# A post-norm transformer layer: the first feed-forward matmul on ternary weights and split activations, and a new order of the small pieces

## The chip, the core and the metric

One core of one Trainium2 chip. The metric is the device time of one execution, in microseconds, as the median of several. All input tensors start in device memory (HBM), and the output of shape 8 x 1024 x 256, fp32, ends there. The names used below: PE is the matmul engine (PEld its weight loads), DVE the vector engine, ACT the scalar (activation) engine, POOL the general engine, SP the engine whose queue issues nearly all DMAs.

## The reference

```python
# x: 8 x 1024 x 256; 16 heads of 16
Q, K, V = split_heads(x @ Wq.T + bq), split_heads(x @ Wk.T + bk), split_heads(x @ Wv.T + bv)
scores = einsum('bhqd,bhkd->bhqk', Q, K) / sqrt(16) + prior_lambda * gaussian_mask(1024)
out = einsum('bhqk,bhkd->bhqd', softmax(scores), V)       # heads joined again
x = layernorm(x + out @ Wo.T + bo)

def bitlinear(x, w):
    scale = clip(mean(abs(w), axis=1, keepdims=True), 1e-5, None)
    return x @ (clip(round(w / scale), -1, 1) * scale).T
h = bitlinear(x, w_fc) + gate * (x @ v.T @ fast_b.T @ u.T)  # w_fc 1024 x 256; rank 16
r = maximum(h, 0)
x = layernorm(x + bitlinear(r * r, w_proj))                 # w_proj 256 x 1024
```

So the first feed-forward matmul has two parts. The weights of the large part have only the values -1, 0 and 1, times one scale for each of the 1024 hidden rows. The second part goes through rank 16.

## The kernel before

**Groups.** The attention runs in 512 groups, 64 for each of the 8 batches. In one group PE forms two score tiles that are ready for the exponential (`exp_scores`, L684; matmuls at L699), then some other pieces of work, then the four matmuls (L629, `max_scores`) whose row maxima are needed 12 groups later, and at last the product of the previous group's exponentials with V (L738, `weigh`). In five of eight groups the Gaussian mask touches the tile: there the first of the two tiles gets four matmuls with the mask (L709), and DVE adds it to the second (L722). ACT takes the exponentials (L723). DVE takes the row maxima, two for each group, 1024 columns each (L641, `max_row`); one of them is queued before the pieces' results are taken out of PSUM, the other only in the next group. Scores live in three PSUM tiles of two banks each that are taken in turn.

**Pieces.** Everything else is cut into pieces that a scheduler in Python puts into the groups while the program is built: for the batch after, `transpose_x`, `queries_keys` and `values`; for the batch before, the feed-forward part in four chunks of 256 rows (`chunk`, L819). A chunk is two `project` pieces (output projection, residual, statistics of the norm), two `turn` pieces (transposing x), eight `hidden` pieces (first feed-forward matmul, L884), and four half `output` pieces (L918). A piece writes half a PSUM bank, `misc`, of which there are two halves, so that a group takes two such pieces at most. A piece is a tuple: an assumed PE cost, the function, the number of halves, and a condition. The loop at L1072 pays out credit: each group gets its share of the batch's total cost, and pieces are taken while there is credit. `defer(n, f)` puts work n groups later; it is issued by `run_deferred` (L1133), before the pieces' results are taken.

**What is computed how.** Matmul operands of type F32R go through PE once, plain F32 operands in several passes (two records in the trace for each matmul). The scores and the second feed-forward matmul already use pairs of F32R numbers, the value rounded and the rest. The first feed-forward matmul is plain F32: `prepare_fc` (L407) forms in batch 0 the whole weight, ternary value times scale plus the low-rank product, in `wfT`; `hidden` multiplies it with `x1T`. The square of the relu is then split in `hi` and `lo`: ACT relu (L896) and square (L900), POOL multiplication (L901) and subtraction (L903; on DVE in the last batch).

**Queues.** All instructions of an engine run in the order in which they were issued (L1146 to L1151 add that dependency). SP's DMAs stand in one such order too: the q and k parts (L189 to L196), the row maxima's round trip through HBM (L671, L677), the sums and outputs of the attention (L756, L759), the steps of the softmax normalization (L764 to L793: `sums`, `invert`, `fetch`, `divide`, deferred by 1, 2, 3 and 4 groups) and the loads.

**Tail.** After group 511 the last batch's feed-forward part runs alone (L1139), on the score tiles' PSUM banks, which `early` (L363) hands out in pairs.

Of the kernel before, what the change touches and what calls it, by code (L numbers as in the profile page):

```python
# [16 lines left out]
P = 128  # L17
# [21 lines left out]
def tile_postln_layer(  # L39
# [82 lines left out]
    ones = cpool.tile([P, P], F32, tag="ones", name="ones")  # L122
# [97 lines left out]
    for name in "kq":  # L220
# [3 lines left out]
        p1.tile([P, HALF], F32, tag="full", name="full_0"),  # L224
        p1.tile([P, HALF], F32, tag="avs", name="full_1"),
        p2.tile([P, HALF], F32, tag="rl", name="full_2"),
        p2.tile([P, HALF], F32, tag="rl", name="full_3"),
# [5 lines left out]
    first_part("q", qscale, 0, "rec", fulls[1])  # L233
# [95 lines left out]
    gate_c = cpool.tile([R, 1], F32, tag="gate", name="gate_c")  # L329
    nc.sync.dma_start(gate_c, gate.partition_broadcast(R))  # L330
    fb_sb = cpool.tile([R, R], F32, tag="fb", name="fb_sb")
    nc.sync.dma_start(fb_sb, fast_b)
    v_sb = cpool.tile([R, D], F32, tag="v_sb", name="v_sb")
    nc.sync.dma_start(v_sb, v)
    u_sb = cpool.tile([P, NHC, R], F32, tag="u_sb", name="u_sb")
# [48 lines left out]
    wfT = cpool.tile([P, NDC, FF], F32, tag="wfT", name="wfT")  # L384
# [3 lines left out]
    def scales(w, n, name):  # L388


        sc = p2.tile([P, 3], F32, tag="sc", name=f"sc_{name}")
        nc.vector.tensor_reduce(
            out=sc[:, 0:1], in_=w, axis=AX.X, op=ALU.add, apply_absolute_value=True
        )
        nc.vector.tensor_scalar(sc[:, 0:1], sc[:, 0:1], 1.0 / n, 1e-5, op0=ALU.mult, op1=ALU.max)
        nc.vector.tensor_scalar_mul(sc[:, 1:2], sc[:, 0:1], 0.5)
        nc.vector.tensor_scalar_mul(sc[:, 2:3], sc[:, 0:1], -0.5)
        return sc

    def ternary(w, sc, name):  # L400

        t = p1.tile([P, D], F32, tag="tern", name=f"tern_{name}")
        nc.gpsimd.tensor_scalar(t, w, sc[:, 2:3], None, op0=ALU.is_lt)
        nc.gpsimd.tensor_scalar(w, w, sc[:, 1:2], None, op0=ALU.is_gt)
        nc.gpsimd.tensor_sub(w, w, t)

    def prepare_fc(half):  # L407

# [25 lines left out]

        def second():
            st["a"] = p1.tile([R, HALF], F32, tag="lo", name=f"a_{half}")
            pas = [misc(f"pa_{half}_{k}") for k in range(2)]
            for k, pa in enumerate(pas):
                nc.tensor.matmul(
                    pa[:R, :], fb_sb, st["uT"][:, ts(k, D)], start=True, stop=True  # L440
                )

            def empty():
# [12 lines left out]
        def piece(i):  # L456
# [13 lines left out]
            def empty():  # L470
# [3 lines left out]
                if i + 1 < n:  # L474
                    tern(i + 1)
# [723 lines left out]
```

## Time and profile before

Three runs took 2405.73, 2407.56 and 2408.98 us, median 2407.56. The profiled execution took 2407.72 us, of which 2405.8 us are the span from the first to the last instruction.

| stretch of the span (us) | what runs | length | PE busy | DVE busy | ACT busy | POOL busy | PE clock |
|---|---|---|---|---|---|---|---|
| 0 to 70 | weights, first q, k, v, first maxima | 70 | 46.96 | 41.69 | 12.62 | 23.88 | 0.79 |
| 70 to 332 | batch 0, and preparing the feed-forward weights | 262 | 244.14 | 196.39 | 143.60 | 63.33 | 0.98 |
| 604 to 883 | batch 2 | 279 | 274.79 | 197.51 | 162.16 | 93.53 | 0.99 |
| 1716 to 1998 | batch 6 | 282 | 277.04 | 198.36 | 162.24 | 93.54 | 0.99 |
| 1998 to 2267 | batch 7 | 269 | 260.50 | 168.55 | 159.31 | 92.33 | 0.99 |
| 2320 to 2347 | tail, second chunk | 27 | 18.33 | 7.98 | 6.11 | 13.62 | 0.81 |

Busy is the time in which an engine had at least one instruction in work. The clock is what was granted to PE, as a share of full speed. The costs of instructions that the change touches, as the page's groups give them (busy us in all, mean ns of one): L884 228.8 and 383 (896 records), L896 on `misc` 83.5 and 382 (224), L850 23.2 and 415 (56), L594 18.3 and 611 (30 each for q and k), L789 40.3 and 1281 (32). PE, DVE and the others wait for each other through semaphores; in the profile a wait stands as idle time before an instruction, with the instruction that ended it.

### The profile page before, as it was taken

What the parts mean: (1) busy time and instruction counts of PE and PEld (TensorE: products, weight loads), DVE (VectorE), ACT (ScalarE), POOL (GpSimd) and SP (SyncE); (2) the same over time, 40 slices, a digit from 0 to 9 for tenths busy, and PEclk for the clock granted to TensorE, in tenths of its full rate; (3) what the DMA queues carried; (4) which work ended last, traced back from release to release, by engine and by line L of the source; (5) the groups of instructions that cost most, each with busy time, mean ns of one, the idle gap of its engine ahead of it and who ended that gap; (6) DMA issues with size and microseconds to landing.
All of it is one profiled execution on the core that took longest, in us unless ns stands there. A gap on an engine that the chain in (4) does not pass through costs nothing.

```text
span 2405.8 us, 35921 instructions
## 1 busy us (share of the span) xinstructions
PE 2269.3 (94%) x12956; PEld 1302.4 (54%) x12956; DVE 1623.2 (67%) x3117; ACT 1312.0 (55%) x1748; POOL 790.1 (33%) x796
## 2 busy tenths in 40 slices
PE   6899999999999999999999999999999999999666
PEld 4444445555555555555555555555555555555344
DVE  6677777777677777677676776777766777776122
ACT  1455565655555565665556555555655556555421
POOL 3124112323223342333324332333323333333344
PEclk8899999999999999999999999999999999999878
DMA  8223343231423323132423223233332124221100
GB/s 207 74 66 102 73 110 100 63 77 44 130 85 83 86 79 112 56 84 69 119 85 102 68 55 111 86 85 79 94 111 65 59 73 117 65 50 33 37 13 18
DMA packets 108433, 194.06 MB, mean 81 GB/s; under 512 B 20944, under 2 KB 49888, under 8 KB 108256
## 3 DMA queue, kind: packets, MB, share of 16 engines
q1 hardware_dynamic: 106848, 189.68, 28.7%
q10 hardware_dynamic: 1408, 2.10, 0.3%
q8 instruction: 102, 1.67, 0.3%
q14 instruction: 75, 0.61, 0.1%
HBM read 105.73 MB, written 85.98 MB: 80 GB/s over the span
## 4 chain that ended last, share of the span: by engine, by line
PE 76%; DVE 10%; DMA 5%; POOL 3%; issue 3%; ACT 1%; SPq 1%; POOLq 0%; DVEq 0%; ACTq 0%
PE e L699 19%; PE av L738 16%; PE s L629 14%; PE misc L884 7%; DVE junk L641 7%; PE e L709 5%; PE misc L918 5%; PE misc L575 4%; DMA o<-raw_o 2%; PE misc L553 2%; PE misc L841 2%; DVE st L798 1%; DMA st_q<-parts_q 1%; PE py L918 1%; PE ph L884 1%
## 5 line engine op out<-in xcount | busy, mean ns | idle before, releaser
L641 DVE CUSTOM_DVE_ANT_0 junk<-s,wide 128x1024 f32<-128x1024 f32 x1024 | 1248.9, 1220 | 591.8 <-PE s L629 553.8
L723 ACT ACTIVATE exp<-e 128x1024 f32<-128x1024 f32 x1024 | 1023.1, 1024 | 752.5 <-PE e L709 512.0
L699 PE MATMUL e<-st_q,st_k 66*128 66x512 f32 (+1 forms) x2048 | 680.2, 428 | 8.7 <-DMA st_q<-rows 6.6
L699 PEld LDWEIGHTS e<-st_q,st_k 66*128 66x128 f32 (+1 forms) x2048 | 321.0, 189 | 468.0 <-issue 137.8
L738 PE MATMUL av<-exp,v 128*17 128x512 f32 x4096 | 541.4, 600 | 0.0
L629 PE MATMUL s<-st_k,st_q 64*128 64x512 f32 x2048 | 403.6, 451 | 39.0 <-DVE pm L641 31.7
L629 PEld LDWEIGHTS s<-st_k,st_q 64*128 64x128 f32 x2048 | 166.7, 187 | 201.1 <-DVE pm L641 98.8
L884 PE MATMUL misc<-x1T,wfT 128*128 128x256 f32 x896 | 228.8, 383 | 5.4 <-ACT rl L896 4.5
L901 POOL TENSOR_TENSOR rl<-rl 128x512 f32<-128x512 f32 x128 | 133.2, 1041 | 286.7 <-ACT hi L900 285.8
L709 PEld LDWEIGHTS e<-prior,ident_r 128*128 128x128 f32 x1280 | 194.4, 191 | 29.3
L722 DVE TENSOR_TENSOR e<-e,wide 128x372 f32<-128x372 f32 (+2 forms) x320 | 174.0, 544 | 47.3 <-PE e L699 39.6
L938 POOL TENSOR_TENSOR r<-r,x 128x256 f32<-128x256 f32 x64 | 47.1, 736 | 435.0 <-DVE r L937 435.0
L884 PEld LDWEIGHTS misc<-x1T,wfT 128*128 128x128 f32 x896 | 167.1, 191 | 41.3 <-ACT rl L896 7.6
L709 PE MATMUL e<-prior,ident_r 128*128 128x186 f32 (+2 forms) x1280 | 187.8, 269 | 0.0
L738 PEld LDWEIGHTS av<-exp,v 128*17 128x17 f32 x4096 | 68.1, 95 | 187.1 <-issue 184.6
L805 POOL TENSOR_TENSOR rstd<-ve,mhalf 128x2 f32<-128x2 f32 x64 | 45.6, 713 | 359.4 <-DVE ve L803 354.8
L903 POOL TENSOR_TENSOR lo<-rl,hi 128x512 fp32r<-128x512 f32 x112 | 143.3, 1280 | 8.8
L896 ACT ACTIVATE rl<-misc 128x256 f32<-128x256 f32 x224 | 83.5, 382 | 61.5 <-DVE both L662 37.5
L918 PE MATMUL misc<-wpT,hi 128*128 128x256 f32 x448 | 117.0, 295 | 0.0
L918 PE MATMUL misc<-wpT,lo 128*128 128x256 f32 x448 | 113.2, 286 | 0.5 <-POOL lo L903 0.5
L789 POOL TENSOR_TENSOR o<-o,rec 128x512 f32<-128x512 f32 x32 | 40.3, 1281 | 165.4 <-DMA o<-raw_o 142.8
L918 PEld LDWEIGHTS misc<-wpT,hi 128*128 128x128 f32 x448 | 87.2, 195 | 5.2 <-DVE both L662 1.1
(146 smaller groups left out, 1795.7 us busy)
## 6 DMA issues: line engine op xcount, KB each, us to landing
st_k<-parts_k SPq DMA_DIRECT2D x128, 256.0 KB
st_q<-parts_q SPq DMA_DIRECT2D x124, 256.0 KB
parts_k<-twok SPq DMA_DIRECT2D x60, 512.0 KB
parts_q<-twoq SPq DMA_DIRECT2D x64, 256.0 KB
parts_q<-twoq SPq DMA_DIRECT2D x30, 512.0 KB
x<-in_L_attn_x_dram SPq DMA_DIRECT2D x16, 512.0 KB
raw_o<-avs SPq DMA_DIRECT2D x256, 32.0 KB
x<-in_L_attn_x_dram SPq DMA_DIRECT2D x32, 256.0 KB
```

What stands on the lines that cost most here:

```text
L575: nc.tensor.matmul(pt, wT[name][:, dc, ts(c, P)], xT[:, dc, ts(2 * half + k, D)], start=(dc == 0), stop=(dc == NDC - 1),)
L629: nc.tensor.matmul(pair[a][:, kh, :], stack["q", s, pr, a][rows, ts(blk, P)], stack["k", s, pr, a][rows, ts(kh, HALF)], start=True, stop=True,
L641: nc.vector.tensor_tensor_reduce(out=junk, in0=t.rearrange("p k n -> p (k n)"), in1=wide[:, LEFT - P * blk : LEFT - P * blk + L], scale=1. ...
L699: nc.tensor.matmul(t[:, a, :], stack["k", s, pr, a][rows, ts(blk, P)], stack["q", s, pr, a][rows, ts(h, HALF)], start=True, stop=not (near ...
L709: nc.tensor.matmul(t[:, a, lo - HALF * h : hi - HALF * h], ident_r, prior[:, n, lo - first : hi - first], start=False, stop=(n == 1),)
L722: nc.vector.tensor_add(part, part, add.to_broadcast([P, 2, hi - lo]))
L723: nc.scalar.activation(e, t.rearrange("p a n -> p (a n)"), AF.Exp)
L738: nc.tensor.matmul(av[32 * j : 32 * j + HD + 1, :], v_bufs[b % 2][:, blk, g * HG + j, : HD + 1], es[j // 2][:, ts(j % 2, HALF)], start=(n ...
L884: nc.tensor.matmul(ph, wfT[:, dc, ts(hc, P)], st["x1T"][:, dc, :], start=(dc == 0), stop=(dc == NDC - 1),)
L901: nc.gpsimd.tensor_mul(rl, rl, rl)
L903: sub(lo, rl, hi.bitcast(F32))
L918: nc.tensor.matmul(py, st[k][:, hc, ts(i, P)], wpT[:, hc, :], start=(hc == 0 and k == "hi"), stop=(hc == NHC - 1 and k == "lo"),)
```

## The change

Seven things are edited.

1. `wfT` holds the ternary values alone. The scale of each hidden row is a column of `s_fc` and is applied by the relu. x is split in `turn` into two F32R numbers, `xhi` (rounded) and `xlo` (the rest), and `hidden` multiplies both.
2. The low-rank part is a matmul of its own: a piece `low_rank` for each chunk multiplies x with `v_st` (v, split, repeated to 128 columns), and its result, split again, is the operand of a fifth matmul in `hidden`, against `lowT` (the rows of gate times u times fast_b, divided by the scale).
3. `prepare_fc` is cut differently for that, with a new `prepare_v`; `ternary` compares w times two with the scale.
4. In `queries_keys` the rounding copy moves from POOL to ACT, and its buffer `full` becomes one of the two of tag `rl`.
5. The softmax normalization is deferred by 1, 3, 4, 6 and 8 groups and works in two halves.
6. The statistics of the first norm are deferred; `run_deferred` is called after the pieces' results are taken.
7. The scheduler: pieces stand in another order, and credit is gone. A group takes pieces until their cost is above 0.75, and one more only when the batch's remaining groups are short.

```diff
     def ternary(w, sc, name):
         t = p1.tile([P, D], F32, tag="tern", name=f"tern_{name}")
-        nc.gpsimd.tensor_scalar(t, w, sc[:, 2:3], None, op0=ALU.is_lt)
-        nc.gpsimd.tensor_scalar(w, w, sc[:, 1:2], None, op0=ALU.is_gt)
+        nc.gpsimd.tensor_scalar(t, w, -2.0, sc, op0=ALU.mult, op1=ALU.is_gt)
+        nc.gpsimd.tensor_scalar(w, w, 2.0, sc, op0=ALU.mult, op1=ALU.is_gt)
         nc.gpsimd.tensor_sub(w, w, t)
...
+        def tern(i, pf):
+            w, hc = st["w"][:, i, :], n * half + i
+            sc = s_fc[:, hc : hc + 1]
+            scales(sc, w, D)
             ternary(w, sc, f"fc_{half}_{i}")
-            nc.gpsimd.tensor_scalar_mul(w, w, sc[:, 0:1])
+            full = p1.tile([P, R], F32, tag="lowf", name=f"lowf_{half}_{i}")
+            nc.scalar.copy(full, pf)
+            def rows():
+                inv = p2.tile([P, 1], F32, tag="inv", name=f"inv_{half}_{i}")
+                nc.vector.reciprocal(inv, sc)
+                nc.vector.tensor_scalar(full, full, inv, gate_c, op0=ALU.mult, op1=ALU.mult)
+                low = ones_low[:, 1, :].rearrange("p (a b c r) -> p a b c r", a=2, b=2, c=2)
+                for k in range(2):
+                    src = full.unsqueeze(1).to_broadcast([P, 2, R])
+                    nc.vector.tensor_copy(low[:, k, 0].bitcast(F32R), src)
+                    nc.vector.tensor_sub(low[:, k, 1], src, low[:, k, 0])
+                st["rows"] = i
+            defer(1, rows)
...
-                to = wfT[:, :, ts(n * half + i, P)]
-                nc.scalar.copy(to, pw.rearrange("p (c h) -> p c h", h=P))
-                nc.vector.tensor_add(to, to, pl.rearrange("p (c h) -> p c h", h=P))
+                at = ts(n * half + i, P)
+                nc.scalar.copy(wfT[:, :, at], pw.rearrange("p (c h) -> p c h", h=P))
+                nc.scalar.copy(lowT[:, at], pl[:, :P])
...
-                    st["full"] = p1.tile(
-                        [P, HALF], F32, tag="full", name=f"full{name}_{b}_{c}_{half}"
+                    st["full"] = p2.tile(
+                        [P, HALF], F32, tag="rl", name=f"full{name}_{b}_{c}_{half}"
                     )
...
-                nc.gpsimd.tensor_copy(two[:, 0, :], full)
+                nc.scalar.copy(two[:, 0, :], full)
                 nc.gpsimd.tensor_sub(two[:, 1, :], full, two[:, 0, :].bitcast(F32))
...
+        def divide(half):
+            o = o_of[b, c][:, ts(half, HALF)]
+            nc.gpsimd.tensor_mul(o, o, st["rec"])
+            if half + 1 < NHALF:
+                fetch(half + 1)
+            else:
+                divided.add((b, c))
-        for k, f in enumerate((sums, invert, fetch, divide)):
-            defer(k + 1, f)
+        steps = {1: sums, 3: invert, 4: lambda: fetch(0), 6: lambda: divide(0), 8: lambda: divide(1)}
+        for n, f in steps.items():
+            defer(n, f)
...
             def empty():
-                nc.scalar.copy(st["x1T"][:, dc, :], pt)
+                nc.scalar.copy(st["xhi"][:, dc, :], pt)
+                nc.vector.tensor_sub(st["xlo"][:, dc, :], pt, st["xhi"][:, dc, :].bitcast(F32))
                 st["turned"] = dc + 1
...
+        def low_rank():
+            pt = bank(f"plow_{b}_{c}")
+            for dc in range(NDC):
+                for k in ("xhi", "xlo"):
+                    nc.tensor.matmul(
+                        pt, v_st[:, dc, :], st[k][:, dc, :],
+                        start=(dc == 0 and k == "xhi"), stop=(dc == NDC - 1 and k == "xlo"),
+                    )
+            def empty():
+                t = p1.tile([P, n], F32R, tag="tern", name=f"low_{b}_{c}")
+                nc.scalar.copy(t, pt)
+                lower = t[P // 2 :]
+                nc.vector.tensor_sub(lower, pt[P // 2 :], lower.bitcast(F32))
+                st["low"] = t
+            return empty
...
             for dc in range(NDC):
-                nc.tensor.matmul(
-                    ph, wfT[:, dc, ts(hc, P)], st["x1T"][:, dc, :],
-                    start=(dc == 0), stop=(dc == NDC - 1),
-                )
+                for k2 in ("xhi", "xlo"):
+                    nc.tensor.matmul(
+                        ph, wfT[:, dc, ts(hc, P)], st[k2][:, dc, :],
+                        start=(dc == 0 and k2 == "xhi"), stop=False,
+                    )
+            nc.tensor.matmul(ph, lowT[:, ts(hc, P)], st["low"], start=False, stop=True)
...
-                nc.scalar.activation(rl[:, ts(k, n)], ph, AF.Relu)
+                nc.scalar.activation(rl[:, ts(k, n)], ph, AF.Relu, scale=s_fc[:, hc : hc + 1])
...
+                res += [with_(load, h[0]), *h[1:3], with_(bias, h[3]), *nxt[:2], *h[4:], *more]
+                res += [*o[:2], nxt[2], *o[2:], *nxt[3:5], *end]
...
+                elif filled > 0.75 and not (spare < (-1 if near(g) else 2)):
                     break
...
-        run_deferred(g)
         for empty in empties:
             if empty is not None:
                 empty()
+        run_deferred(g)
...
-    for u in [gap] * 5 + feed_forward(B - 1, early) + [gap] * 2:
+    for u in [gap] * 8 + feed_forward(B - 1, early) + [gap] * 2:
```

At the start of the program, the rounded and rest parts of the first q half take the buffer of tag `junk` (the scratch output of the row maxima) instead of that of tag `rec`, and `v_sb`, `u_sb` and the first fp32 copies take buffers of tags that are used later.

## The prediction

> **What bounds the kernel now.** I read the page first: its engines, its forty slices, its chain. The columns are busy us, share of the span, instructions; below, the costliest groups with count, busy us, mean ns, and idle time with its releasers.
>
> ```profile
> span 2405.8 us, 35921 instructions
> PE 2269.3 (94%) x12956; PEld 1302.4 (54%) x12956; DVE 1623.2 (67%) x3117; ACT 1312.0 (55%) x1748; POOL 790.1 (33%) x796
> ...
> PE   6899999999999999999999999999999999999666
> ...
> PE 76%; DVE 10%; DMA 5%; POOL 3%; issue 3%; ACT 1%; SPq 1%; POOLq 0%; DVEq 0%; ACTq 0%
> ...
> L884 PE MATMUL misc<-x1T,wfT 128*128 128x256 f32 x896 | 228.8, 383 | 5.4 <-ACT rl L896 4.5
> ```
>
> PE is the bound from slice 3 to slice 37, but 94% busy doesn't say that each microsecond of PE work costs one. The PE timeline does (start us, length us, group):
>
> ```profile
> 1202.25 1.20 PE L699 MATMUL e<-st_q,st_k 66*128 66x512 f32 x4
> 1203.29 1.02 PE L575 MATMUL misc<-xT,wkT 128*128 128x256 f32 x4
> 1204.25 0.73 PE L629 MATMUL s<-st_k,st_q 64*128 64x512 f32 x4
> 1204.91 1.05 PE L738 MATMUL av<-exp,v 128*17 128x512 f32 x8
> 1205.89 0.74 PE L699 MATMUL e<-st_q,st_k 66*128 66x512 f32 x2
> ...
> 1210.92 1.21 PE L699 MATMUL e<-st_q,st_k 66*128 66x512 f32 x4
> 1211.97 0.28 PE L918 MATMUL misc<-wpT,hi 128*128 128x256 f32 x1
> 1212.09 0.28 PE L918 MATMUL misc<-wpT,lo 128*128 128x256 f32 x1
> ```
>
> One group is e, pieces, s, av; a "near" group (five of eight) adds four prior matmuls. I cut the whole timeline where L699 follows L738: 512 groups, the first at 70.31, the last at 2263.83. From group 64 on their medians are: near with two 256-column fp32 pieces (hidden, projection, q/k or v) 4.96, with one 4.10, with none 3.92; far 4.51, 3.65, 3.55 (3.50 with two turns). The step from one to two pieces is 0.86, so PE's own part is 4.96 - 1.72 = 3.24 near and 4.51 - 1.72 = 2.79 far. The step from none to one is only 0.18 or less: below about 0.7 us of pieces a group stands on a **floor**, 3.92 or 3.50, set by other engines (two row maxima of 1.22 on DVE and the scores between them). So a group takes the larger of its floor and 3.24 (or 2.79) plus its pieces. Other pieces by the same differences: half an output (eight L918) 0.93, a turn 0.22, the maximum's transpose 0.11.
>
> For groups 128 to 191 this gives 272.8 us, measured 279.1; for groups 64 to 510 it leaves 45.6 us unexplained, which are stalls.
>
> **Part 1: the hidden piece.** Removed: two fp32 matmuls (four records, 0.86). Added: five fp32r matmuls of 256 columns, four with x's halves and one with the low-rank rows. No such matmul with wfT was run; the nearest row is L918, same operand kind and shape, start to start 0.12 above, so 5 x 0.12 = 0.60. A chunk also gets one low-rank piece, 4 x 0.12 = 0.48. Per chunk of 8 hidden pieces: 8 x 0.26 - 0.48 = 1.6 us less PE work, 6.4 for a batch's four.
>
> A rule speaks against this. The Trainium skill, "TensorE: Matmul & The Clock Gate", section "Measured speedup vs the span model", says that a weight load overlaps a running matmul only when the row groups differ. All five loads here fill all rows. By it each matmul would pay its load and its stream, 0.19 + 0.11, the hidden piece would be 1.5 us, and 256 of them would add 164 us. The rows (PEld is the weight load):
>
> ```profile
> 1212.20 0.28 PE L918 MATMUL misc<-wpT,hi 128*128 128x256 f32 x1
> 1212.21 0.19 PEld L918 LDWEIGHTS misc<-wpT,lo 128*128 128x128 f32 x1
> 1212.32 0.28 PE L918 MATMUL misc<-wpT,lo 128*128 128x256 f32 x1
> ```
>
> The 0.19 us load begins 0.01 after a full-row matmul and the next matmul starts 0.11 later: it overlaps. I take 0.12.
>
> **Part 2: the order of pieces.** A lone hidden piece of 0.60 would lie under the floor and waste 0.08, so it matters that the changed kernel's PE order, counted from the built program, mostly has two in a group: 3.24 + 1.20 = 4.44 near, 3.99 far. For groups 128 to 191 (40 near, 24 far): own parts 40 x 3.24 + 24 x 2.79 = 196.6 in both; pieces 74.3 before, 67.9 after; unfilled floors 1.9 (5 groups) before, 2.7 (7 groups) after. Sums 272.8 and 267.2: **-5.6**. The same count gives -5.7 for batch 1, -5.6 for each of batches 2 to 6, and -5.7 for batch 7 (whose last twelve groups have no s). Groups 64 to 510: **-39.4**. Batch 0 has no hidden piece.
>
> **Part 3: normalization later, in halves.** The steps move from groups +1, 2, 3, 4 to +1, 3, 4, 6, 8. Today the division stands at POOL's head while its data is in flight:
>
> ```profile
> 621.64 0.40 SPq L784 DMA_DIRECT2D o<-raw_o  x1
> ...
> 629.70 2.52 POOL L789 TENSOR_TENSOR o<-o,rec 128x512 f32<-128x512 f32 x2 [9.51 <-DMA o<-raw_o]
> ...
> 639.82 0.47 PE L699 MATMUL e<-st_q,st_k 66*128 66x512 f32 x1 [1.65 <-DMA st_q<-rows]
> ```
>
> POOL idles 142.8 us over 14 such waits. Behind it stand L595's subtraction, on it SP's write of q parts (634.18), behind that the row maxima's DMA (635.90), and then PE. Groups 7 and 8 of the batches lose 11.3 us to this, group 55 twice 1.8, group 502 6.3 (there the residual add and the norm stood behind the division). Sum 19.4. Two groups between fetch and division are about 8 us, the 8 us that the o transfer took at 621.64. The second half's fetch waits on SP for the first division (1.28), with only q/k writes, the next x load and row DMAs behind it. Bounds 0 and -22; I take **-16**, since the fetch now shares the queue with the row DMAs one group later.
>
> **Part 4: what ACT, DVE and POOL get.** ACT: 60 casts of q/k parts come from POOL (128x512; nearest L749, 0.58 us: 35 us), 32 low-rank copies (12 us), and a scale column on the relu (between L896's 0.38 and L590's 0.47: 0 to 23 us). ACT goes from 1312 to about 1380 and stays under 60%. A cast that waits for its buffer now blocks the exponentials, but POOL's casts waited for that DMA only at the start. DVE: 64 subtractions for xlo and 32 for the low-rank rows, like L850's 0.42 at most: 40 us, to about 70%. They wait for an ACT copy and stand before the group's second maximum. Hidden in groups with PE slack; bounds 0 and 96 x 0.42 = +40. Nearest is a pair of turns, 3.98 against 3.92 with none, 0.06 each: **+5**. POOL loses 60 casts (0.61), gains nothing. Cover gone, each of these costs its length.
>
> **Part 5: start and preparation.** The first q parts now sit in the buffer of the first maximum's scratch output, which must wait for their DMA (issued until 33.64; the maximum started at 34.04): about +2.5. The q/k buffer is double now, so the 3.1 us for which DVE idled at 62.55 behind an ACT result should shrink: -3, zero together. In batch 0 PE waited 3.7 for POOL's ternary rows; the new condition gives it a group of distance, while small DVE operations are added. Bounds -6 and +6, taken **-2**.
>
> **Part 6: the tail** runs from group 511 to the end, 142 us, with these stretches (us, then PE, PEld, DVE, ACT, POOL busy, clock):
>
> ```profile
> 2267.00:2294.00 27.00, 5.22 (x14) 2.09 (x12) 2.79 (x8) 0.79 (x2) 5.89 (x6) 0.62 0.29 66
> 2294.00:2320.00 26.00, 17.20 (x64) 11.76 (x64) 6.25 (x12) 6.86 (x16) 11.90 (x12) 0.81 0.00 0
> 2347.00:2376.00 29.00, 21.20 (x76) 15.95 (x76) 7.43 (x18) 6.11 (x14) 13.61 (x14) 0.71 0.06 19
> ```
>
> No engine is full; handoffs set it. 32 hidden pieces x 0.26 = -8.3, low-rank +1.9, the first projection needs one divided half (-1.3), and in the first chunk the path copy, subtraction, four matmuls, copy, subtraction stands bare: 0.37 + 0.42 + 0.48 + 0.37 + 0.42 = +2.1. In later chunks it lies beside POOL's norm (2.43). Sum -5.6, **-6**; bounds +8 (all paths bare, PE's gain lost in waits) and -14 (the 4.5 us waits at the shared bank go).
>
> **Sum.** -39.4 - 16 + 5 - 2 - 6 = -58.4. The profiled run has span 2405.8 and took 2407.72, practically the shown median 2407.56: 2405.8 - 58.4 + 1.9 = **2349 us**.
>
> **Rivals.**
> - Stalls move, they don't vanish: only parts 1, 2, 4 and 5 count, the tail gives nothing. -36.4: 2371. For it: 26 of the 45.6 us of stalls have no cause named here. Against: the POOL wait is plain.
> - More goes: stalls fall by 32, tail by 14, part 4 is free: -87, 2320. For it: the L884 waits in the tail hang on buffers that are paired anew.
> - Slower: q/k's full tile now shares the two buffers of rl, and in a batch one tile is held from the seventh to the eighth q/k piece, across four hidden pairs. These then pass through one buffer: relu, square, POOL's multiply and subtraction (0.38 + 0.38 + 0.63 + 1.04 + 1.28 = 3.7 us) against a group of 4.0 to 4.4. A norm on POOL in front (2.43) holds relu and, through the pieces' bank, PE. 28 pairs wait in seven batches; from 58 / 28 = 2.1 us each the gain is gone. With norm and bias add (1.5) each time, 28 x 3.9 = 109: 2458. Against: POOL is 33% busy.
> - It doesn't do what it says: the fp32r stream runs at load plus stream, above 2500; the L918 rows exclude it nearly.
>
> **How the numbers follow.** Forecast 0.60, stalls move 0.20, more goes 0.10, slower 0.08, not as said 0.02. A measurement here tells 0.2% (4.8 us) from none. Faster: 0.60 + 0.20 + 0.10, less 0.01 for a part of the second case that ends at zero: 0.89. Same 0.03, slower 0.08. Range: forecast's own bounds 2330 to 2366, widened to 2325 and 2380 to take in the second case and half of the third: about 0.8.
>
> **What would show it.** Right: L943/L950 spaced 0.12; near groups with two hidden pieces at 4.44; no POOL wait of 9 us before the division; group 8's wait for rows under 1 us. Wrong: hidden pairs above 4.7, relu waiting for POOL's subtraction, or many turn groups above 4.2.

## The result and the profile after

Four runs took 2375.04 to 2377.29 us, median 2375.98. Four runs of the kernel before took 2405.73 to 2408.98, median 2406.94. The ratio is 0.9871, with a 95% interval from 0.9854 to 0.9888: 1.3% faster, 31 us, where 58 were forecast. The time is 27 us above the forecast, and 5 us from the rival "stalls move, they don't vanish" (2371). It lies inside the stated range, but 10 us above the forecast's own bounds (2330 to 2366).

The page of the changed kernel, its parts 1, 2, 4 and 5 (busy us, share and instructions; forty slices; chain; groups). New line numbers: L652 is the old L629 (`max_scores`), L664 the old L641 (`max_row`), L722 and L732 the score tile and its mask, L943 and L950 `hidden`, L956 its relu.

```profile
span 2374.1 us, 36785 instructions
PE 2230.5 (94%) x13328; PEld 1301.7 (55%) x13328; DVE 1665.6 (70%) x3233; ACT 1377.8 (58%) x1856; POOL 756.4 (32%) x728
...
PE   6998999999999999999999999999999999999676
...
PE 72%; DVE 14%; issue 2%; ACT 2%; POOL 1%; DMA 0%; POOLq 0%; SPq 0%; ACTq 0%; DVEq 0%
...
L943 PE MATMUL misc<-xhi,wfT 128*128 128x256 f32 x448 | 117.0, 284 | 1.9 <-DVE low L929 1.0
...
L956 ACT ACTIVATE rl<-misc,s_fc 128x256 f32<-128x256 f32 x224 | 93.9, 474 | 10.5 <-DVE both L685 4.9
```

PE has 38.8 us less work, and the span is only 31.7 us shorter, so PE waits more than before. In the chain PE falls from 76% to 72%, DMA from 5% to 0, and DVE rises from 10% to 14%.

The new matmuls do what the forecast said. The PE timeline in one group (start us, length us):

```profile
1040.35 0.28 PE L943 MATMUL misc<-xhi,wfT 128*128 128x256 f32 x1
1040.47 0.28 PE L943 MATMUL misc<-xlo,wfT 128*128 128x256 f32 x1
1040.59 0.28 PE L943 MATMUL misc<-xhi,wfT 128*128 128x256 f32 x1
```

They follow each other at 0.12 us. Cut into the same 512 groups, the timeline gives 4.40 for a near group with two hidden pieces (forecast 4.44), 3.95 for a far one (3.99), and 4.01 for a near group with one turn (the forecast had 3.98 for two; a single near group has two turns now, 3.97). The parts of the span, in us:

| stretch | before | after | difference |
|---|---|---|---|
| to the first group | 70.31 | 71.47 | +1.2 |
| groups 0 to 63 (batch 0) | 262.2 | 258.8 | -3.4 |
| groups 64 to 510 | 1931.3 | 1893.8 | -37.5 |
| tail, from group 511 | 142.0 | 150.0 | +8.0 |
| span | 2405.8 | 2374.1 | -31.7 |

For groups 64 to 510 the rule of the forecast (the larger of the floor and PE's own part plus pieces) alone gives -39.4. What lies above the rule was 45.6 us before and is 47.5 us now, so stalls have not become fewer. They stand elsewhere. This is the mean over batches 2 to 6 of the stall above the rule, in us for one group, by the group's number in its batch (17 and 18 summed):

| group | 7 | 8 | 17, 18 | 6 | 11 | 21 | 27 | 37 | 38 | 56 | 59 | 61 | 62 |
|---|---|---|---|---|---|---|---|---|---|---|---|---|---|
| before | 1.37 | 0.96 | 0.85 | 0 | 0 | 0 | 0 | 0 | 0 | 0 | 0 | 0.17 | 0 |
| after | 0 | 0 | 0 | 0.53 | 0.79 | 1.71 | 0.65 | 0.67 | 0.65 | 0.38 | 0.34 | 0.57 | 0.41 |

The table leaves out smaller ones: before, groups 13, 25, 40, 52, 54 and 55 had 0.19 to 0.48 each, and have 0.12 at most now. In all, a batch's stalls were 5.7 us and are 7.1.

The stalls at groups 7 and 8 are gone, as part 3 said. In the view of the tile `o`, the time for which POOL idled before the division until o's data came was, in the kernel before and in the changed one (us, times):

```profile
  DMA o<-raw_o: 142.8, 14
```

```profile
  DMA o<-raw_o: 14.4, 2
```

But PE's view of waits shows s waiting longer for the row maxima on DVE (us in all, times, longest), first before, then after:

```profile
PE s L629 <- DVE pm L641: 31.7, 65, 2.1
```

```profile
PE s L652 <- DVE pm L664: 56.1, 91, 5.1
```

**What holds up the maxima.** The timeline of the changed kernel in group 21 of batch 3:

```profile
957.57 1.23 DVE L664 CUSTOM_DVE_ANT_0 junk<-s,wide 128x1024 f32<-128x1024 f32 x1 [1.00 <-PE s L652]
...
959.10 1.29 POOL L618 TENSOR_TENSOR twok<-fullk,twok 128x512 fp32r<-128x512 f32 x1 [31.18 <-ACT twok L617]
959.18 0.18 DVE L828 BATCH_NORM_AGGREGATE mv<-st 128x2 f32<-128x6 f32 x1
959.39 1.02 DVE L832 TENSOR_SCALAR ve<-mv 128x2 f32<-128x2 f32 x1
960.33 1.21 DVE L664 CUSTOM_DVE_ANT_0 junk<-s,wide 128x1024 f32<-128x1024 f32 x1
...
961.61 1.21 PE L652 MATMUL s<-st_k,st_q 64*128 64x512 f32 x4 [1.61 <-DVE pm L664]
```

L832 adds epsilon to two variances per partition, 256 numbers in all. It takes 1.02 us and ends at 960.41, 0.02 after POOL's subtraction L618 (960.39). The group's second maximum stands behind it, and s behind that: PE idles for 1.61. Elsewhere L832 takes 0.17, as the view of tile `ve` shows (min/median/max in ns), before and after:

```profile
L803 DVE TENSOR_SCALAR ve<-mv x64: 168/169/819, 385.4 to 2399.0; 128x2 f32<-128x2 f32 x64
```

```profile
L832 DVE TENSOR_SCALAR ve<-mv x64: 169/170/1025, 399.4 to 2367.3; 128x2 f32<-128x2 f32 x64
```

Before, 3 of its 64 cases were long. Now 27 are (0.55 to 1.02), each with a POOL instruction in work as it starts, and each ends 0.02 to 0.03 us after that one. In batches 2 to 6 they are those of groups 11, 21, 33 and 56 (0.88, 1.02, 0.56, 0.70), and all but group 33 have a stall in the table. The sum of the extra lengths is 16.4 us.

A second kind of stall is at group 27. Its timeline has part 4's subtraction for the low-rank rows (L929), the copy of a q/k piece (L613) and the moved cast (L617):

```profile
984.94 1.23 DVE L664 CUSTOM_DVE_ANT_0 junk<-s,wide 128x1024 f32<-128x1024 f32 x1 [1.38 <-PE s L652]
...
986.20 0.43 DVE L929 TENSOR_TENSOR low<-misc,low 64x256 fp32r<-64x256 f32 x1
986.66 1.23 DVE L664 CUSTOM_DVE_ANT_0 junk<-s,wide 128x1024 f32<-128x1024 f32 x1
986.66 0.47 ACT L613 ACTIVATE fullk<-misc,bk 128x256 f32<-128x256 f32 x1 [1.73 <-DVE low L929]
987.21 0.62 ACT L617 CAST twok<-fullk 128x512 fp32r<-128x512 f32 x1
987.74 1.93 ACT L746 ACTIVATE exp<-e 128x1024 f32<-128x1024 f32 x2
```

The subtraction stands between the two maxima. By the profile ACT's copy waits 1.73 for it, then the cast runs, and only then come the exponentials. So the second maximum is late by the subtraction's 0.43, and the exponentials by more.

**The tail.** The window of the whole tail, before and after (us; PE, PEld, DVE, ACT, POOL busy; PE clock):

```profile
2263.80:2405.80 142.00, 79.65 (x332) 56.57 (x328) 33.45 (x77) 27.11 (x60) 58.74 (x60) 0.77 0.09 24
```

```profile
2224.06:2374.10 150.04, 88.96 (x396) 71.55 (x392) 37.89 (x92) 32.06 (x63) 62.48 (x63) 0.66 0.08 23
```

PE's busy time rises by 9.3 us there, where the forecast booked 6.4 less work. The granted clock falls from 0.77 to 0.66, and most of the new matmuls follow each other at 0.21 us instead of the loop's 0.12. In the chain that ended last, PE stands for 52.5 us of the tail before and for 63.8 after, more than any other engine.

### The profile page after: what moved, and what is told of

Its sections match the earlier page's. It is cut to its first block, busy times and chain, and to the rows that moved or that the text cites. A ratio compares the mean times of both kernels' runs of the same rounds, so it can differ in the third digit from the quotient of the medians.

```text
span 2374.1 us, 36785 instructions
## 1 busy us (share of the span) xinstructions
PE 2230.5 (94%) x13328; PEld 1301.7 (55%) x13328; DVE 1665.6 (70%) x3233; ACT 1377.8 (58%) x1856; POOL 756.4 (32%) x728
## 4 chain that ended last, share of the span: by engine, by line
PE 72%; DVE 14%; issue 2%; ACT 2%; POOL 1%; DMA 0%; POOLq 0%; SPq 0%; ACTq 0%; DVEq 0%
PE e L722 18%; PE av L761 15%; PE s L652 14%; DVE junk L664 9%; PE e L732 4%; PE misc L943 4%; PE misc L978 4%; PE misc L598 3%; PE misc L870 2%; PE misc L576 2%; PE misc L950 1%; DVE st L827 1%; DVE ve L832 1%; PE ph L943 1%; DVE mv L828 1%
## 5 line engine op out<-in xcount | busy, mean ns | idle before, releaser
L664 DVE CUSTOM_DVE_ANT_0 junk<-s,wide 128x1024 f32<-128x1024 f32 x1024 | 1248.4, 1219 | 523.0 <-PE s L652 485.1
L722 PE MATMUL e<-st_q,st_k 66*128 66x512 f32 (+1 forms) x2048 | 680.1, 428 | 0.9 <-DVE pm L664 0.7
L722 PEld LDWEIGHTS e<-st_q,st_k 66*128 66x128 f32 (+1 forms) x2048 | 320.8, 190 | 460.0 <-ACT exp L746 138.1
L652 PE MATMUL s<-st_k,st_q 64*128 64x512 f32 x2048 | 411.8, 452 | 63.6 <-DVE pm L664 56.1
L652 PEld LDWEIGHTS s<-st_k,st_q 64*128 64x128 f32 x2048 | 169.8, 187 | 211.2 <-DVE pm L664 126.6
L961 POOL TENSOR_TENSOR rl<-rl 128x512 f32<-128x512 f32 x128 | 133.3, 1041 | 461.4 <-ACT hi L960 421.7
L732 PEld LDWEIGHTS e<-prior,ident_r 128*128 128x128 f32 x1280 | 194.4, 191 | 29.6
L732 PE MATMUL e<-prior,ident_r 128*128 128x186 f32 (+2 forms) x1280 | 187.9, 269 | 0.0
L618 POOL TENSOR_TENSOR twok<-fullk,twok 128x512 fp32r<-128x512 f32 x30 | 38.8, 1292 | 384.4 <-ACT twok L617 354.4
L943 PE MATMUL misc<-xhi,wfT 128*128 128x256 f32 x448 | 117.0, 284 | 1.9 <-DVE low L929 1.0
L943 PE MATMUL misc<-xlo,wfT 128*128 128x256 f32 x448 | 115.0, 280 | 0.0
L978 PE MATMUL misc<-wpT,hi 128*128 128x256 f32 x448 | 114.7, 291 | 0.2 <-DVE xlo L907 0.2
L978 PE MATMUL misc<-wpT,lo 128*128 128x256 f32 x448 | 110.5, 282 | 1.7 <-POOL lo L963 1.7
L956 ACT ACTIVATE rl<-misc,s_fc 128x256 f32<-128x256 f32 x224 | 93.9, 474 | 10.5 <-DVE both L685 4.9
L618 POOL TENSOR_TENSOR twoq<-fullq,twoq 128x512 fp32r<-128x512 f32 x30 | 38.8, 1295 | 176.7 <-ACT twoq L617 176.7
L943 PEld LDWEIGHTS misc<-xhi,wfT 128*128 128x128 f32 x448 | 84.4, 188 | 12.7 <-DVE low L929 3.7
```

Of the source, the lines that this page charges most:

```text
L652: nc.tensor.matmul(pair[a][:, kh, :], stack["q", s, pr, a][rows, ts(blk, P)], stack["k", s, pr, a][rows, ts(kh, HALF)], start=True, stop=True,
L664: nc.vector.tensor_tensor_reduce(out=junk, in0=t.rearrange("p k n -> p (k n)"), in1=wide[:, LEFT - P * blk : LEFT - P * blk + L], scale=1. ...
L722: nc.tensor.matmul(t[:, a, :], stack["k", s, pr, a][rows, ts(blk, P)], stack["q", s, pr, a][rows, ts(h, HALF)], start=True, stop=not (near ...
L732: nc.tensor.matmul(t[:, a, lo - HALF * h : hi - HALF * h], ident_r, prior[:, n, lo - first : hi - first], start=False, stop=(n == 1),)
L943: nc.tensor.matmul(ph, wfT[:, dc, ts(hc, P)], st[k2][:, dc, :], start=(dc == 0 and k2 == "xhi"), stop=False,)
L956: nc.scalar.activation(rl[:, ts(k, n)], ph, AF.Relu, scale=s_fc[:, hc : hc + 1])
```

## Experiments

The theory after the first reading had three parts. In the loop, what part 4 called small (L832 beside POOL, the subtractions before the second maximum, the cast on ACT) makes the new stalls. In the tail, the added hops copy, subtraction, matmul cost more than the PE work saved. The rivals were the normalization's new distance, the low PE clock of the tail, and the order of the pieces itself. Each kernel ran beside the kernel before. The changed kernel ran again as a yardstick for these runs.

> The changed kernel as it is, as the yardstick of the runs beside it: about 2376, a ratio of 0.987 to the kernel before.

It took 2376.62 us (2376.1 to 2378.5), ratio to before 0.9848 (0.983 to 0.9867), span 2375.1, tail 150.3. In the different sets of runs the medians of the kernel before lay between 2406.9 and 2413.7, so a difference of medians from different sets is good to some 0.3%, or 7 us; the stretches within a profile say more. Differences below are against this run, and differences of stretches against the first profile (loop means groups 64 to 510, 1893.8; tail 150.0).

**1. Without the rest of x.** The two subtractions on DVE are left out: a tile of zeros stands for xlo, and the second half of the low-rank rows stays the rounded value. PE does the same matmuls.

```diff
-                for k, tag in (("xhi", "x1T"), ("xlo", "x1lo")):
-                    st[k] = p1.tile([P, NDC, n], F32R, tag=tag, name=f"{k}_{b}_{c}")
+                st["xhi"] = p1.tile([P, NDC, n], F32R, tag="x1T", name=f"xhi_{b}_{c}")
+                if not zero_rest:
+                    zero_rest.append(p1.tile([P, NDC, n], F32R, tag="x1lo", name="zero_rest"))
+                    nc.gpsimd.memset(zero_rest[0].bitcast(F32), 0.0)
+                st["xlo"] = zero_rest[0]
...
-                nc.vector.tensor_sub(st["xlo"][:, dc, :], pt, st["xhi"][:, dc, :].bitcast(F32))
...
-                nc.vector.tensor_sub(lower, pt[P // 2 :], lower.bitcast(F32))
```

> The changed kernel without the two DVE subtractions: the rest of x is left zero, and the second half of the low-rank rows is the rounded value again; PE runs the same matmuls in the same order. Theory A (the new stalls come from DVE work that stands between a group's two row maxima, and from ACT, which waits for it): of each batch's groups, numbers 27, 37, 38 and 61 lose their 0.55 to 0.67 us over the floor-and-pieces sum, 2.5 us a batch, 18 in seven, and the four tail chunks lose 0.5 to 1 each: about 2355. Theory B (the stalls come from the q and k casts on ACT): those groups keep them, 2373 to 2376.

2348.86 us (2346.42 to 2349.98), 27.8 less. The loop is 18.2 shorter, the tail 8.9 (141.1). The stalls at groups 27, 38, 59 and 62 are gone (all within 0.04), and those at 37 and 61 fall from 0.67 and 0.57 to 0.23 and 0.22. Groups 11 and 21 stay. So the subtractions (84 of the 96 are in the loop) cost 18 us there. The tail without them is about as long as before the change (142.0). But its granted clock is 0.71 instead of 0.66, and PE is busy for 80.85 us instead of 88.96. So the 8.9 us are the subtractions and a faster PE together, and this run doesn't separate the two.

**2. The cast back on POOL.**

```diff
-                nc.scalar.copy(two[:, 0, :], full)
+                nc.gpsimd.tensor_copy(two[:, 0, :], full)
```

> The rounding copy of q and k goes back from ACT to POOL, all else as changed. Theory B: the exponentials of groups 6 and 27 no longer wait for the cast; both lose about 0.5 us over the sum, seven times: 7 us, 2369. Theory A: POOL's queue gets 0.6 us longer sixty times and ACT's shorter, nothing is gained: 2374 to 2378.

2370.71 us (2369.15 to 2372.73), 5.9 less; loop -5.2. Group 6 falls from 0.53 to 0.10, group 27 from 0.65 to 0.39. The cast costs little on POOL. On ACT it stands before exponentials that are needed at once.

**3. The normalization sooner again**, in halves as in the change:

```diff
-        steps = {1: sums, 3: invert, 4: lambda: fetch(0), 6: lambda: divide(0), 8: lambda: divide(1)}
+        steps = {1: sums, 2: invert, 3: lambda: fetch(0), 4: lambda: divide(0), 5: lambda: divide(1)}
```

> The normalization's steps at 1, 2, 3, 4 and 5 groups instead of 1, 3, 4, 6 and 8, still in two halves; same order on PE. If the later steps are what took the old stalls away (the prediction's part 3), POOL waits for the o transfer again for several us, and groups 7 and 8 of the batches lose 1 us or more again: plus 8 to 16, 2384 to 2392. If the new order of pieces took them away, 2375 to 2378.

2385.2 us (2384.55 to 2385.61), 8.6 more: loop +5.2, of it 4.6 in the last 63 groups, and tail +4.3. Groups 7 and 8 stay without a stall. So in the changed kernel the distance brings 8.6 us, and it is not what emptied groups 7 and 8 there. Halves and the new order together did that; they were not run apart.

**4. Epsilon added on POOL** instead of DVE, the one instruction L832:

```diff
-        nc.vector.tensor_scalar_add(ve, mv[:, :, 1], EPS)
+        nc.gpsimd.tensor_scalar(ve, mv[:, :, 1], EPS, None, op0=ALU.add)
```

> The addition of epsilon to the variance (128 x 2) goes from DVE to POOL, which takes the root right after it. In the changed kernel this DVE instruction takes 0.17 us mostly, but 0.55 to 1.02 in 26 of 64 cases, each time while a POOL multiplication or subtraction runs. Theory D (it waits for POOL at a shared port and holds the second row maximum behind it): groups 11 and 21 lose 0.7 to 1 us over the sum, seven times, and POOL's extra 0.2 us costs nothing: minus 8 to 14, about 2365. If the long duration is only recorded so and holds nobody: 2375 to 2378.

2354.71 us (2354.32 to 2356.2), 21.9 less; loop -20.4. Groups 11, 22 and 56 are at 0, group 21 falls from 1.71 to 0.23. The same group of the same batch in its timeline:

```profile
952.40 1.29 POOL L618 TENSOR_TENSOR twok<-fullk,twok 128x512 fp32r<-128x512 f32 x1 [31.17 <-ACT twok L617]
952.47 0.18 DVE L828 BATCH_NORM_AGGREGATE mv<-st 128x2 f32<-128x6 f32 x1
952.57 1.19 DVE L664 CUSTOM_DVE_ANT_0 junk<-s,wide 128x1024 f32<-128x1024 f32 x1
953.66 0.23 POOL L832 TENSOR_SCALAR ve<-mv 128x2 f32<-128x2 f32 x1
...
953.83 0.73 PE L652 MATMUL s<-st_k,st_q 64*128 64x512 f32 x4 [0.54 <-DVE pm L664]
```

POOL's subtraction is as long as before, the maximum beside it too. What is gone is the 1.02 us in front of it, and PE's wait falls from 1.61 to 0.54. 55 of the 64 cases are in the loop. The gain stands where L832 was long: of the 3.3 us that a batch loses (mean of batches 2 to 6), 2.9 are at groups 11, 21, 22 and 56. The other 0.5 are at groups 37 and 61, where L832 took its 0.17 and is now gone from DVE. An estimate from these two: some 0.2 us at each of groups 11, 21 and 56 would have gone with the short instruction alone, so about two thirds of the loop's gain, 13 us, are the lengthening beside POOL.

**5. PE kept warm at the start of the tail**: useless fp32 matmuls in two of the gaps where PE waits anyway.

```diff
+    fill = {8: 28, 16: 12}      # before the first projection, before the first turn
+    def warm(n):
+        for _ in range(n):
+            nc.tensor.matmul(two_halves[:, 0, :], woT[:, 0, :P], woT[:, 1, :], start=True, stop=True)
...
+        if k in fill:
+            warm(fill[k])
```

> The changed kernel with 28 useless fp32 matmuls of 256 columns in the tail before the first projection, where PE waits 14 us anyway, and 12 before the first turn, where it waits 4; nobody reads their result. Theory C (part of the tail's loss is PE's clock: from 2244 to 2287 it was granted 0.50 and 0.56, the L943 are spaced 0.21 instead of 0.12): the clock in these stretches rises above 0.8 and the first chunk loses 4 to 8 us, 2368 to 2372. Theory A for the tail (the chain over ACT and DVE sets it, and PE's clock lies in its shadow): 2374 to 2378.

2376.04 us (2374.4 to 2377.14), the same within 0.6; the profiled tail is 2.8 shorter, and its profile is of the fastest of the four runs. The windows of the first chunk, about up to the first hidden matmul and up to the second chunk's (us; PE, PEld, DVE, ACT, POOL busy; PE clock), in the changed kernel and then in this one:

```profile
2244.00:2258.00 14.00, 6.49 (x15) 3.53 (x15) 4.11 (x10) 1.12 (x3) 4.62 (x5) 0.50 0.13 37
2258.00:2287.50 29.50, 22.43 (x89) 18.91 (x90) 8.39 (x20) 7.05 (x14) 12.26 (x13) 0.56 0.00 1
```

```profile
2245.00:2259.00 14.00, 10.83 (x42) 8.32 (x43) 3.52 (x10) 1.12 (x3) 4.83 (x5) 0.88 0.13 37
2259.00:2288.00 29.00, 19.25 (x92) 15.96 (x90) 8.82 (x21) 7.44 (x15) 13.64 (x14) 0.70 0.00 1
```

The clock rises from 0.50 to 0.88 and from 0.56 to 0.70. The second chunk's first hidden matmul starts 61.3 us after group 511 instead of 63.4, so the first chunk gains 2.1 us where theory C asked for 4 to 8. Behind it the extra matmuls no longer help: the three windows up to the end have 0.66, 0.75 and 0.63, in the changed kernel 0.79, 0.68 and 0.62. So a slow PE is a small part of the first chunk's length; what it costs in the later chunks this run doesn't show.

**6. A PSUM tile for each piece in the tail.** In the changed kernel two pieces of the tail share a score tile, and its timeline shows what that does:

```profile
2279.39 0.37 ACT L906 CAST xhi<-ptx 128x256 fp32r<-128x256 f32 x1 [4.30 <-PE ptx L903]
...
2280.80 0.39 DVE L907 TENSOR_TENSOR xlo<-ptx,xhi 128x256 fp32r<-128x256 f32 x1
2281.24 0.38 PE L978 MATMUL ptx<-wpT,hi 128*128 128x256 f32 x1 [1.90 <-DVE xlo L907]
```

An output piece (L978) writes the other half of the tile `ptx` and waits 1.90 for the subtraction that reads the first half. This kernel makes two edits at once: `early` gives each piece a tile of its own, and in the tail the next chunk's two turns come together after two half outputs, its low-rank piece between the last two.

```diff
-        if not pair_of:
-            t = se(name)
-            pair_of.extend((t[:, 0, :D], t[:, 1, :D]))
-        return pair_of.pop(0)
+        return se(name)[:, 0, :D]
...
-                res += [*o[:2], nxt[2], *o[2:], *nxt[3:5], *end]
+                if bank is early:
+                    res += [*o[:2], *nxt[2:4], o[2], nxt[4], o[3], *end]
+                else:
+                    res += [*o[:2], nxt[2], *o[2:], *nxt[3:5], *end]
```

> The tail alone is changed: each piece has a PSUM tile of its own (three in turn, instead of six halves that share a tile by two), and a chunk's two turns and its low-rank piece are spread between the four half outputs, so that copies and subtractions run beside output matmuls. The loop is untouched. If the two subtractions and the waits at shared tiles make the tail longer (150.0 us against 142.0 before the change): it loses 2 to 3 us a chunk, about 140 us, 2366. If the tail is set by POOL and the clock: within 3 us, 2373 to 2379.

2354.87 us (2353.98 to 2358.34), 21.8 less. The tail falls to 128.2, a larger gain than either forecast named, and the loop is unchanged (1894.0). The tail's clock is 0.77, and PE's part of its chain falls from 63.8 to 25.1 us.

**7. The same, tiles alone, on the kernel before.**

> The kernel before the change, with a PSUM tile for each piece of the tail and nothing else. If tiles that two pieces share cost the tail time already before the change (PE waits of 4.5 us for the residual add, at hidden pieces that share its tile): 8 to 14 us less. If they hurt only with the new order: within 3 us.

2392.03 us (2387.76 to 2395.1), ratio to before 0.9928 (0.9911 to 0.9944). The tail falls from 142.0 to 121.2. So sharing cost 21 us before the change already, and seems not to be the cause of its +8.0: with own tiles the tail is 121.2 before and 128.2 after, still +7.0. The comparison isn't clean, since experiment 6 also moved the turns.

**8. The later normalization alone, on the kernel before**, without halves:

```diff
-        for k, f in enumerate((sums, invert, fetch, divide)):
-            defer(k + 1, f)
+        for k, f in zip((1, 3, 4, 6), (sums, invert, fetch, divide)):
+            defer(k, f)
...
-    for u in [gap] * 5 + feed_forward(B - 1, early) + [gap] * 2:
+    for u in [gap] * 8 + feed_forward(B - 1, early) + [gap] * 2:
```

> The kernel before the change, with the normalization's steps at 1, 3, 4 and 6 groups and nothing else (three more empty steps ahead of the tail). The prediction's part 3 on its own: groups 7, 8, 55 and 502 lose their waits of 19 us in sum, 2388 to 2393. If it was the new order of pieces that removed them: less than 6 us, 2401 to 2408.

2393.0 us (2388.83 to 2395.76), ratio 0.9913 (0.9894 to 0.9932), which is 20.3 below the kernel before in the same set of runs. Against the first profile the span is 15.8 shorter, the loop 17.3 (batch 0 gives 2.5 back). Groups 7 and 8 go from 1.37 and 0.96 to 0.

**9. The subtractions behind the second maximum.** If their place before it is the fault, they should do no harm after it. Their issue is put off to the next group, behind its delayed maximum:

```diff
-                nc.vector.tensor_sub(st["xlo"][:, dc, :], pt, st["xhi"][:, dc, :].bitcast(F32))
-                st["turned"] = dc + 1
+                def subtract():
+                    nc.vector.tensor_sub(st["xlo"][:, dc, :], pt, st["xhi"][:, dc, :].bitcast(F32))
+                    st["turned"] = dc + 1
+                late(subtract, bank)        # issued after the next max_row; low likewise
```

> The changed kernel; in the loop the two subtractions (xlo, low-rank rows) are issued after the second row maximum, at the start of the next group, where the ACT copy that they read is long done; nothing is left out, PE's pieces keep their order, the tail is untouched. Theory A in its narrow form (it is not the 0.42 us of the subtraction, but its wait for ACT, in front of the second maximum and with ACT's next copy behind it): groups 27, 37, 38, 59, 61 and 62 lose most of their 3.3 us a batch, about 20 us, 2357. If it is the DVE work itself: it only moves, 2370 to 2380. The half bank is given back later, which can cost up to 0.5 us where two pieces follow.

2441.96 us (2439.18 to 2444.58), ratio to before 1.013 (1.0115 to 1.0145): 65 us slower than the changed kernel. PE's waits show why:

```profile
PE misc L994 <- DVE xlo L917: 15.9, 15, 1.2
PE misc L688 <- DVE xlo L917: 15.3, 12, 1.4
PE misc L928 <- DVE xlo L917: 12.9, 14, 1.2
PE misc L959 <- DVE low L943: 12.1, 14, 1.1
PE misc L911 <- DVE xlo L917: 8.4, 11, 1.0
```

The piece's half of `misc` comes back a maximum later, and the next pieces stand before it on PE. These five rows alone are 64.6 us, as much as the loss; in the changed kernel the waits of PE at `misc` for xlo and low are 2.1 us in all. Neither forecast came: the stalls at groups 27, 37, 38, 59, 61 and 62 grew, to 0.95 to 1.73. The place before the maximum costs 18 us, the place after it far more. A third place was not tried.

**10. Single hidden pieces instead of pairs.** The scheduler's bounds are moved so that a hidden piece counts as a full one:

```diff
-        return sum(1.0 if u[0] > 0.7 else 0.5 if u[0] > 0.5 else 0.0 for u in jobs)
+        return sum(1.0 if u[0] > 0.5 else 0.0 for u in jobs)
...
-                elif filled > 0.75 and not (spare < (-1 if near(g) else 2)):
+                elif filled > 0.55 and not (spare < (-1 if near(g) else 2)):
```

> The changed kernel, with a limit under which one hidden piece fills a group unless the batch runs short; the pieces and their number stay. Counted from the built order, the rule of floor and pieces gives 9.6 us more over the seven batches (1.2 to 1.8 each), 2386 by the rule alone. If pairing decides more than the floor says (the 0.60 piece costing a whole group's 0.86): 2395 and more. If it doesn't matter: 2374 to 2378. New places for stalls can add to each of these.

2409.63 us (2405.4 to 2413.12, 12 runs), ratio to before 0.9985 (0.9974 to 0.9996), 33 us above the changed kernel. By the rule the unfilled floors are worth 9.6 us of these. The rest is stalls, 10.4 us a batch instead of 7.1, at new places: group 18 has 1.92, 45 and 52 have 1.34 and 1.35, while 6, 11 and 27 have none. So the order of the pieces decides where stalls arise, and this new order brought more than it removed. That was the mechanism of the rival at 2371.

**11. The three gains together** (4, 2 and 6):

> The changed kernel with three edits at once: epsilon added on POOL, the cast of two back on POOL, and in the tail a tile for each piece with the part matmuls taken up in the order of the changed list. Theory that the three stalls are separate (VectorE's small instruction kept out beside POOL in the loop, the cast ahead of the exps in the loop, shared tiles in the tail): the gains add, 21.9 + 5.9 + 21.8 = 49.6 us below the changed kernel, some 2327 us, stalls of about 3 us a batch of 64 groups and a tail of 128 us. Rival, that stalls replace one another (POOL gets back the cast and gains the epsilon, so its work stands in the way of the masks elsewhere): 2335 to 2355 us, with the tail at 128 us and the stalls of a batch at 4 us or more.

2330.51 us (2329.35 to 2332.09), ratio to before 0.9673 (0.9657 to 0.969), the fastest kernel here. It is 46.1 below the changed kernel by the medians, 45.5 by the spans; the sum of the three is 49.6. The loop is 24.4 shorter (20.4 + 5.2 = 25.6 alone), the tail 128.6. From its page, the engines and the slices:

```profile
span 2329.6 us, 36899 instructions
...
PE   6899999999999999999999999999999999999855
```

A batch's stalls are 3.2 us instead of 7.1. Of these, 2.6 stand at groups 27, 37, 38, 59, 61 and 62, where the subtractions are, and no version here takes them away with the computation kept.

## Why the prediction was right, and where it was wrong

| part | forecast | measured | from |
|---|---|---|---|
| 1 and 2, hidden piece and order | -39.4 | -39.4 | not measured apart: the rule, which its medians 4.40 and 3.95 fit within 0.04 |
| 3, normalization | -16 | -17.3 | loop of experiment 8 |
| 4, ACT, DVE and POOL | +5 | +19.2 | what is left of the loop's -37.5, all other stalls with it |
| 5, start and batch 0 | -2 | -2.2 | +1.2 - 3.4 |
| 6, tail | -6 | +8.0 | the stretches |
| sum | -58.4 | -31.7 | |

**Parts 1 and 2 held.** The rule fits where no stall is, and the matmuls are spaced 0.12. The 164 us of the rule weighed there don't appear. (That rule stands in the page's section "The mechanism", above the one that the prediction names.)

**Part 3 held in size**, by a run on the kernel before. In the changed kernel undoing the distance costs only 8.6, so the gains don't add as the sum assumed: halves and order seem to cover a part of the same stall.

**Part 4 failed, by a term that wasn't in it and one that was mis-sized.** The work was counted well: DVE 1665.6 busy (+42 against 40 forecast), ACT 1377.8 (forecast 1380). What a subtraction costs was taken from near groups with a pair of turns, 3.98 against 3.92, 0.06 each. Cut again, the 15 such groups have a median of 4.01, which would have given +8, still too little. The subtractions cost 18.2 us, 0.22 for each of the loop's 84 on average, and not evenly. They stand in twelve groups of a batch. In six they are free within 0.1, in the other six they cost 0.3 to 0.7; at group 27 it is seen how: DVE's subtraction stands behind the first maximum, and the second maximum and ACT's copy behind the subtraction. The missing term is L832, 20.4 us. The forecast gave each instruction a fixed length and looked only at what it adds; it did not ask beside which POOL instruction an old one would now stand. The Trainium skill, "SBUF — State Buffer", section "Who interferes with whom", says that a `tensor_scalar` of DVE can need the port pair which it shares with POOL, and that the one that comes first has the pair for its whole instruction while the other "**fully blocks**". The 27 long cases agree, each ending 0.02 to 0.03 after POOL's. So do four short ones (0.17), where POOL's multiplication L961 began 0.01 later than L832; one short case of the kernel before is nearly a tie, with POOL 0.004 ahead. The page would have warned; the rows before showed it too, in the 819 ns maximum of L803 behind a median of 169. The three removals, 20.4 + 18.2 + 5.2 = 43.8, are more than part 4's +19.2. The rest fits the old stalls that went beside those of groups 7 and 8 (17, 18, 25, 40, 52 and others): 3 us a batch by the mean of batches 2 to 6, an estimate of 21 for seven. Which step took them away is not separated.

**Part 6 had the wrong sign.** It booked -8.3 for the hidden pieces and +1.9 for the low-rank ones, and this sum was mis-sized. PE is busy with the hidden pieces for 37.3 us of the tail instead of 42.3, 5.0 less, and with the low-rank ones for 5.5, so nothing is left of the gain. The prices were read in the loop, at a clock of 0.99; the tail has 0.66. Outputs and projections, whose matmuls didn't change, take 41.1 us instead of 31.6 (two more half outputs fall into the stretch). And it put the hops copy, subtraction, matmul at +2.1, in the first chunk alone, with "in later chunks it lies beside POOL's norm". Without the subtractions the tail is 8.9 shorter. How much of this is the hop itself and how much the slower PE that goes with it stays open: the warm start gave back 2.1 in the first chunk, and no run kept PE warm in the later ones. The forecast named the shared bank as a possible gain of 4.5; it was worth 21 already before the change.

**The rivals.** "Stalls move" came within 5 us, with its reason: the sum of the stalls didn't shrink. That it came so close is in part luck: it let part 3 give nothing and the tail stay level, and these errors cancel for the most part: -17.3 against +8.0 in the tail and 14 in part 4. "Slower, through the shared rl buffer" is refuted: in the profile relu waits 3.3 us in all for POOL's subtraction, six times. Of the three signs that would show the forecast wrong, two did not appear (hidden pairs 4.40, turn groups 4.01), and the third, relu waiting for POOL's subtraction, only with these 3.3 us. They were signs of other faults than the ones that came. Direction and range were right, but the range held only because it had been widened to 2380 for the rivals: parts 4 and 6 both missed by 14 us, to the same side.

## What to carry to other kernels

When a change alters the order of work, look in the trace for small instructions whose maximum lies far above their median. Find what runs beside the long ones, because a new order can turn 3 such cases into 27. Price an instruction added ahead of a critical one by the ring of waits that it enters (here copy on ACT, subtraction on DVE, PSUM half back to PE), not by the slack of its engine. In a stretch where no engine is full, don't book saved engine work at the price of a full one: read the clock and the spacing of that stretch, and count the handoffs and the shared buffers.

## What the hardware showed unexpectedly

- An operation on 256 numbers can take six times its time, 1.02 us instead of 0.17, when an instruction of POOL started before it. Other DVE instructions beside the same POOL instructions keep theirs: 28 of 128 BATCH_NORM_AGGREGATEs started beside POOL work and took 0.18, and the 1.2 us row maximum isn't lengthened.
- When an instruction of DVE meets one of POOL, either can be the longer one. DVE's subtraction for `lo` in the tail takes 0.69 us alone and meets POOL in six of its 16 cases. Beside POOL's bias addition that began 0.08 before, it takes 1.20 (two cases). Where the bias addition began 0.22 after it, it stays at 0.69 and the bias addition takes 1.05 instead of 0.74 (one case). Beside POOL's normalization, which began 0.05 before, it stays at 0.69 and the normalization takes 1.76 instead of 1.22 (three of three). That last case doesn't fit "comes first" above, by the starts in the trace; why POOL loses there was not tried. One of the first and one of the last kind:

```profile
2262.72 0.73 POOL L861 TENSOR_TENSOR x<-x,bo_row 128x256 f32<-128x256 f32 x1
2262.80 1.20 DVE L963 TENSOR_TENSOR lo<-rl,hi 128x512 fp32r<-128x512 f32 x1 [4.94 <-POOL rl L961]
...
2273.18 1.76 POOL L839 TENSOR_SCALAR x<-r,mv,rstd 128x256 f32<-128x256 f32 x1
2273.23 0.69 DVE L963 TENSOR_TENSOR lo<-rl,hi 128x512 fp32r<-128x512 f32 x1 [4.06 <-POOL rl L961]
```

- 28 useless matmuls in a gap raised PE's granted clock in the tail's next 14 us from 0.50 to 0.88, and the first chunk became 2.1 us shorter.
- A scale that is a column and not a constant makes the relu 0.474 us instead of 0.382.
